# An LSTM over 512 steps: the output gate's columns computed last and in another PSUM bank, a head of 56 steps, no half cells

## The chip, the cores and the metric

The kernel runs on one core of a Trainium2 chip. A core has five engines with instruction queues of their own that run in order: TensorE (PE, with its weight loads PEld), VectorE (DVE), ScalarE (ACT), GpSimd (POOL) and SyncE (SP), which here starts nearly all DMAs. The metric is the device time of one execution in microseconds (us), lower is better. All data is 32-bit floating point.

## What is computed

An LSTM runs over x (32 sequences, 512 steps, 512 features) from a given state h0; its outputs are added to x. Wx and Wh are 512 x 2048, the four gates i, f, o and g of 512 columns each. Cut to what matters:

```python
xW = jnp.einsum('ntd,dg->ntg', x, Wx) + b
c0 = jnp.zeros_like(h0)

def step(carry, xw_t):
    prev_h, prev_c = carry
    a = xw_t + prev_h @ Wh
    i = jax.nn.sigmoid(a[:, :Hd])
    f = jax.nn.sigmoid(a[:, Hd:2 * Hd])
    o = jax.nn.sigmoid(a[:, 2 * Hd:3 * Hd])
    g = jnp.tanh(a[:, 3 * Hd:])
    next_c = f * prev_c + i * g
    next_h = o * jnp.tanh(next_c)
    return ((next_h, next_c), next_h)
```

The product x Wx does not depend on the recurrence, and can be computed ahead; h Wh can't.

## The kernel before, in words

**A step.** The gates of a step are a PSUM bank of 128 partitions by 512 columns: partition group j (32 partitions, the 32 sequences) holds 128 of each gate's 512 columns. `h_part` (L570) adds h Wh to it with 16 matmuls: four blocks k of the 512 rows by four column groups j of the array, each 512 columns wide; the four of one k run side by side. The trace has two records for each such matmul, for two passes. Two banks, `gates_0` and `gates_1`, alternate by step. `cell` (L592) then applies a sigmoid to i and f (L608), a tanh to g (L609), a sigmoid to o (L610) on ACT; f c, i g and their sum on DVE (L611 to L613); the tanh of c on ACT (L614); o times it on DVE (L615); and a transpose on DVE (L620), which gives ht, the stationary operand of the next `h_part`. POOL adds x for the output (L626). Before that, `seed_gates` (L560) has ACT copy xw, the finished x Wx + b of the step, into the bank, so that the matmuls accumulate on it.

**x Wx.** The first 8 steps are direct (`direct`, L522): 16 matmuls of 512 columns. Five of them run ahead of step 0, three in steps 0 to 2. Steps 8 to 31, the rest of the head (`HEAD`), are made in units (`UNITS`): a unit is 8 steps by 128 columns of each gate and takes, for both halves of the inner dimension, one level of a scheme with 7 products in place of 8. The remaining 480 steps are made in 20 superblocks of 24 steps, each by 20 outer products whose factors are sums of blocks of x and of Wx, and each outer product by the 7 inner ones. A product of the inner level is four matmuls of 256 columns side by side, called a set below: 14 sets make a unit, 140 a superblock.

**Factors.** 14 of the 20 right factors are sums of blocks of Wx. `make_factors` (L181) makes them on DVE in the first steps, two factors behind each cell in steps 0 to 4 and one after that, and SP stores them to memory; `fetch` (L683) loads them again for each superblock.

**Order.** All instructions are written out in a fixed order (L700 on) by time step k and window v; `windows_of(k)` is two windows for each of the first three steps and one for each after. A step issues, in this order: `h_part`; for its window the evacuations of earlier products (`evacuate`: copies on ACT, sums on DVE), planned DVE work (`run_due`), the window's products on PE, the DMAs of `fetch`; then the cell. `run_due` takes work from a list by due window, at most `ROOM` = 3400 columns in a window, each operation counted with 160 more, unless it is overdue. The products of a job are spread over five windows. Superblocks begin in window `START`, which is `LEAD` = 23 steps before the head's end; before this is step 9.

**Half cells.** From `SPLIT` (L551), once all products are made, steps run in halves: each half of the gates' columns has a bank of its own, and the cell is done once per half on half as many columns.

Of the kernel before, what the change touches and what calls it, by code (L numbers as in the profile page):

```python
# [19 lines left out]
H = P // 2  # L20
# [17 lines left out]
HEAD = 4 * ROW  # L38
# [19 lines left out]

START = windows_of(HEAD - LEAD)[0]

# [11 lines left out]
def kernel(  # L72
# [21 lines left out]
    gates = [psum.tile([P, 2, C], F32, name=f"gates_{i}") for i in range(2)]  # L94
# [7 lines left out]
    bias_sb = const.tile([P, 2, C], F32, name="bias_sb")  # L102
# [47 lines left out]
    load_row(3)  # L150
# [30 lines left out]
    def make_factors(n):  # L181
        wa, wb = ring(n, f"make_{n}")
        (first, s0), *rest = B_OF[n]
        assert s0 > 0
        ops = []
        for dst, part in ((wa[:, 0], slice(0, 1)), (wb[:, 0:3], slice(1, 4))):
            dst = dst if part.start else wa[:, 0:1]
            for m, (b, sign) in enumerate(rest):
                src = raw[first][:, part] if m == 0 else dst
                fn = nc.vector.tensor_add if sign > 0 else nc.vector.tensor_sub  # L190
                ops.append(lambda fn=fn, dst=dst, src=src, other=raw[b][:, part]: fn(dst, src, other))  # L191
        ops += [
            lambda: nc.vector.tensor_sub(wa[:, 1], wb[:, 0], wa[:, 0]),
            lambda: nc.vector.tensor_sub(wb[:, 3], wb[:, 2], wb[:, 0]),
            lambda: nc.vector.tensor_sub(wa[:, 2], wb[:, 2], wa[:, 1]),
            lambda: nc.vector.tensor_sub(wb[:, 0], wb[:, 1], wa[:, 2]),
            lambda: nc.sync.dma_start(out=kept[n][0], in_=wa.rearrange("p n c -> p (n c)")),
            lambda: nc.sync.dma_start(out=kept[n][1], in_=wb.rearrange("p n c -> p (n c)")),
        ]
        return ops  # L200

# [319 lines left out]

    def direct(t, bank, qs=range(4)):  # L522
        i, a = divmod(t, ROW)
        for q in qs:
            k, e = divmod(q, 2)
            for j in range(NJ):
                nc.tensor.matmul(
                    bank[j * B : (j + 1) * B].rearrange("p n c -> p (n c)"),
                    rows[i][:, a, q],
                    raw[NJ * k + j][:, 2 * e : 2 * e + 2].rearrange("p n c -> p (n c)"),  # L530
                    start=q == 0,
                    stop=True,
                    skip_group_check=True,
                )

    def keep_direct(t, bank):
        xw[t] = upool.tile([P, 2, C], F32, name=f"xw_{t}", tag="xw", bufs=4)
        nc.vector.tensor_add(xw[t], bank, bias_sb)  # L538

    def load_xw(t):  # L540
        xw[t] = upool.tile([P, 2, C], F32, name=f"xw_{t}", tag="xw", bufs=4)
        i, a = divmod(t, ROW)
        nc.sync.dma_start(out=xw[t].rearrange("p n c -> p (n c)"), in_=stored[i][a])
# [6 lines left out]
    last_window = START + PER * (NSB - 1) + begin(R - 1) + 5  # L550
    SPLIT = next(k for k in range(T) if windows_of(k - 1)[-1] > last_window)  # L551

    def is_split(t):
        return t >= SPLIT

    def half_of(t, i):
        pair = (pps[0], pps[1]) if (t - SPLIT) % 2 == 0 else gates
        return pair[i][:, 0]
# [11 lines left out]
    def h_part(t):  # L570
        if not is_split(t):
            order = [(None, k) for k in range(NJ)]
        else:
            order = [(i, k) for i, ks in ((0, (0, 1)), (1, (0,)), (0, (2, 3)), (1, (1, 2, 3))) for k in ks]
        for i, k in order:
            g = gates[t % 2].rearrange("p n c -> p (n c)") if i is None else half_of(t, i)
            cols = slice(0, 2 * C) if i is None else slice(i * C, (i + 1) * C)
            for j in range(NJ):
                nc.tensor.matmul(  # L579
                    g[j * B : (j + 1) * B],  # L580
                    state["ht"][:, k, :],
                    wh_sb[:, k, j, cols],
                    start=False,
                    stop=True,
                    skip_group_check=True,
                )
# [5 lines left out]
    def cell(t):  # L592
        n, tt = divmod(t, ROW)
        by_half = lambda a: a.rearrange("p (h u) -> p h u", u=H)
        s = work.tile([P, 2, G, H], F32, name=f"s_{t}", tag="s")
# [5 lines left out]
        two = is_split(t)  # L601
        for part in [slice(0, 1), slice(1, 2)] if two else [slice(0, 2)]:
            u = slice(H * part.start, H * part.stop)
            if two:
                g = half_of(t, part.start).rearrange("p (h g u) -> p h g u", h=1, g=G)
            else:
                g = gates[t % 2].rearrange("p h (g u) -> p h g u", g=G)
            nc.scalar.activation(s[:, part, 0:2], g[:, :, 0:2], AF.Sigmoid)  # L608
            nc.scalar.activation(s[:, part, 3], g[:, :, 3], AF.Tanh)  # L609
            nc.scalar.activation(s[:, part, 2], g[:, :, 2], AF.Sigmoid)  # L610
            nc.vector.tensor_mul(by_half(fc[:, u]), s[:, part, 1], by_half(state["c"][:, u]))  # L611
            nc.vector.tensor_mul(by_half(ig[:, u]), s[:, part, 0], s[:, part, 3])  # L612
            nc.vector.tensor_add(c[:, u], fc[:, u], ig[:, u])  # L613
            nc.scalar.activation(tc_t[:, u], c[:, u], AF.Tanh)  # L614
            nc.vector.tensor_mul(by_half(h[:, u]), s[:, part, 2], by_half(tc_t[:, u]))  # L615
            if t == T - 1:
                nc.vector.tensor_add(tc_t[:, u], h[:, u], state["x"][:, u])
                nc.sync.dma_start(out=out[n][:, tt * P + u.start : tt * P + u.stop], in_=tc_t[:, u])
                continue
            nc.vector.transpose(ht[:, 2 * part.start : 2 * part.stop].rearrange("p q b -> p (q b)"), h[:, u])  # L620
        if t == T - 1:
            return
        state["c"], state["ht"] = c, ht
        if tt % 2 == 0:
            state["oc"] = opool.tile([P, 2, NJ, B], F32, name=f"oc_{t}", tag="oc")
        (nc.gpsimd if not two else nc.vector).tensor_add(state["oc"][:, tt % 2], xr[t][:, tt % 2], ht)  # L626
# [9 lines left out]
    for u, (i, j) in enumerate(UNITS):  # L636
# [8 lines left out]
    def prepare(v):  # L645
# [3 lines left out]
        if job is None or job.w >= len(UNITS):  # L649
# [33 lines left out]
    def fetch(v):  # L683
# [9 lines left out]
        sb, rest = divmod(v + 6 - START, PER)  # L693
        if rest < MO and 0 <= sb < NSB:
            load_row(HEAD // ROW + MO * sb + (0, 2, 1)[rest])

    to_make = [n for n in range(R) if len(B_OF[n]) > 1]
    make_at = {k: 2 for k in range(5)}

    with tc.manual_schedule():  # L700
        warm = work.tile([P, G, P], F32, name="warm", tag="s")
        nc.scalar.activation(warm[:, 0], c_init, AF.Sigmoid)
        for m in range(10):
# [8 lines left out]
            bias_sb.rearrange("p n (m l) -> p (n m) l", l=B),  # L712
# [6 lines left out]
        for t in range(2):  # L719
            nc.vector.tensor_add(gates[t], gates[t], bias_sb)  # L720
        for t in range(2, 4):
            keep_direct(t, firsts[t])
        direct(4, pps[2])
        keep_direct(4, pps[2])
# [6 lines left out]
        for k in range(T):  # L731
# [7 lines left out]
            for m, v in enumerate(windows_of(k)):  # L739
                if v == START:  # L740
                    assert not to_make
# [71 lines left out]
```

## Time and profile before

| | us |
|---|---|
| median of 3 runs | 3269.84 (3269.76 to 3272.1) |
| the profiled execution | 3272.06 |
| its span, first to last instruction | 3270.2 |
| PE busy | 3163.7 |
| DVE busy | 2290.2 |
| ACT busy | 1473.4 |
| POOL busy | 931.3 |

The trace has one row per group of like instructions: the start and length in us, the engine, the line of the kernel and the operation, the tile written and those read, the shape, the count, and in brackets how long the engine was idle before and who released it. The end of a matmul in the trace is a model's, some 0.17 us behind the moment at which the next may start; so PE looks busier than it is. In the table of windows a row gives a stretch from a start to an end, its length, each engine's busy time with its count of instructions, the granted clock of TensorE, the share of the DMA engines and the rate.

### The profile page before, as it was taken

The page shows a single profiled execution, that of the slowest core. Times are in us where ns is not written, and L with a number is a line of the kernel's source. Part 1 is how long each engine was busy: PE and PEld are TensorE (multiplying, and loading weights), DVE is VectorE, ACT ScalarE, POOL GpSimd, SP SyncE. Part 2 cuts the span into 40 slices and gives each one's busy share as a digit, 9 for nine tenths or more (in the row PEclk, how much of TensorE's full clock was granted, in tenths as well). Part 3 has the DMA queues.
Part 4 walks back from the last instruction along what each step waited for, and adds up shares of the span by engine and source line. Part 5 has one row for each costly group of instructions (what it writes and reads, how often), then busy time and mean ns, then how long its engine had stood idle before and what let it go on. Part 6 is the DMA issues. An engine that isn't in the chain of part 4 may idle for free.

```text
span 3270.2 us, 101636 instructions
## 1 busy us (share of the span) xinstructions
PE 3163.7 (97%) x40980; PEld 1297.2 (40%) x40980; DVE 2290.2 (70%) x6388; ACT 1473.4 (45%) x4482; POOL 931.3 (28%) x1002
## 2 busy tenths in 40 slices
PE   7899999999999999999999999999999999999987
PEld 2334434434443434434443434444443434344333
DVE  4666776767676777767676777767676767767665
ACT  1344444444444444444444444444444444444434
POOL 0022332323232322323232323323232323323232
PEclk8999999999999999999999999999999999999999
DMA  4466566657566576666566565667566666666552
GB/s 181 157 192 223 179 221 204 221 180 236 182 211 225 171 227 196 221 194 225 177 221 209 191 222 186 219 198 232 171 222 203 200 217 183 220 207 223 174 158 69
DMA packets 324904, 649.79 MB, mean 199 GB/s; under 512 B 43600, under 2 KB 109264, under 8 KB 323920
## 3 DMA queue, kind: packets, MB, share of 16 engines
q1 hardware_dynamic: 324288, 643.28, 61.0%
q8 instruction: 322, 5.28, 0.7%
q14 instruction: 150, 1.23, 0.1%
q10 hardware_dynamic: 144, 0.01, 0.0%
HBM read 464.59 MB, written 178.52 MB: 197 GB/s over the span
## 4 chain that ended last, share of the span: by engine, by line
PE 75%; DVE 12%; issue 5%; ACT 5%; DMA 1%; POOL 1%; SPq 0%; DVEq 0%; ACTq 0%; POOLq 0%
PE gates L579 46%; PE pp L342 12%; PE acc L342 11%; PE p L342 4%; ACT s L608 2%; ACT ig L614 2%; DVE fc L611 2%; DVE ht L620 1%; DVE fc L615 1%; DVE c L613 1%; DVE ig L612 1%; POOL xw L546 1%; DVE wb_make L191 1%; DMA xw<-slot 1%; PE pp L579 1%
## 5 line engine op out<-in xcount | busy, mean ns | idle before, releaser
L579 PE MATMUL gates<-wh_sb,ht 128*32 128x512 f32 (+1 forms) x16352 | 1828.8, 588 | 49.0 <-DVE ht L620 42.1
L579 PEld LDWEIGHTS gates<-wh_sb,ht 128*32 128x32 f32 x16352 | 488.3, 109 | 1136.7 <-issue 883.3
L626 POOL TENSOR_TENSOR oc<-xr,ht 128x128 f32<-128x128 f32 x494 | 297.6, 602 | 2228.4 <-DVE ht L620 2228.4
L608 ACT ACTIVATE s<-gates 128x256 f32<-128x256 f32 (+1 forms) x512 | 194.2, 379 | 1119.3 <-PE gates L579 1119.1
L546 POOL TENSOR_TENSOR xw<-xw,bias_sb 128x512 f32<-128x512 f32 x504 | 651.7, 1294 | 96.1 <-DMA xw<-xw 44.6
L611 DVE TENSOR_TENSOR fc<-s,c 128x128 f32<-128x128 f32 (+1 forms) x529 | 155.7, 294 | 400.4 <-ACT s L608 396.6
L614 ACT ACTIVATE ig<-c 128x128 f32<-128x128 f32 (+1 forms) x530 | 162.0, 306 | 337.5 <-DVE c L613 337.5
L383 DVE TENSOR_TENSOR pp<-acc,p 128x256 f32<-128x256 f32 x412 | 177.7, 431 | 191.7 <-ACT pp L382 176.9
L615 DVE TENSOR_TENSOR fc<-s,ig 128x128 f32<-128x128 f32 (+1 forms) x530 | 153.3, 289 | 221.6 <-ACT ig L614 221.6
L381 ACT COPY pp<-pu 128x512 f32<-128x512 f32 x412 | 247.8, 601 | 125.5 <-DVE slot L489 63.0
L565 ACT COPY gates<-xw 128x512 f32<-128x512 f32 x492 | 285.1, 579 | 34.3 <-DVE xw L538 33.6
L342 PE MATMUL pp<-wb,node 128*32 128x256 f32 x3200 | 247.0, 379 | 0.0
L620 DVE STREAM_TRANSPOSE ht<-fc 128x128 f32<-128x128 f32 (+1 forms) x528 | 162.3, 307 | 56.9 <-DVE fc L615 3.7
L377 DVE TENSOR_TENSOR pu<-acc,p 128x256 f32<-128x256 f32 x412 | 168.8, 410 | 15.9 <-ACT p L374 11.8
L342 PE MATMUL acc<-wa,s 128*32 128x256 f32 x2240 | 173.6, 380 | 2.9
L342 PE MATMUL pp<-wb,s 128*32 128x256 f32 x2240 | 172.7, 379 | 0.0
L342 PE MATMUL acc<-wb,s 128*32 128x256 f32 x2240 | 172.7, 379 | 0.0
L342 PE MATMUL p<-wa,s 128*32 128x256 f32 x2240 | 172.7, 379 | 0.0
L382 ACT COPY pp<-acc 128x256 f32<-128x256 f32 x412 | 148.6, 361 | 43.6 <-DVE slot L489 24.9
L370 ACT COPY pu<-acc 128x256 f32<-128x256 f32 x412 | 151.7, 368 | 31.4 <-PE acc L342 31.4
L613 DVE TENSOR_TENSOR c<-fc,ig 128x128 f32<-128x128 f32 (+1 forms) x530 | 152.3, 287 | 18.4
L374 ACT COPY p<-p 128x256 f32<-128x256 f32 x412 | 154.7, 375 | 5.1 <-PE p L342 5.1
(136 smaller groups left out, 3806.4 us busy)
## 6 DMA issues: line engine op xcount, KB each, us to landing
wb<-keep_b SPq DMA_DIRECT2D x280, 512.0 KB, 5.4
xw<-xw SPq DMA_DIRECT2D x504, 256.0 KB, 3.9
wa<-keep_a SPq DMA_DIRECT2D x280, 384.0 KB, 4.7
xw<-slot SPq DMA_DIRECT2D x488, 128.0 KB, 3.3
xw<-t SPq DMA_DIRECT2D x268, 128.0 KB, 3.4
xr<-in_x_dram SPq DMA_DIRECT2D x256, 128.0 KB, 3.0
out_dram<-oc SPq DMA_DIRECT2D x255, 128.0 KB, 1.9
row<-in_x_dram SPq DMA_DIRECT2D x63, 512.0 KB, 6.6
```

The lines of the kernel that those rows point to most:

```text
L342: nc.tensor.matmul(dst[t * B : (t + 1) * B], a[:, t], w, start=s in (1, 5) and m == 0, stop=True, skip_group_check=True,)
L381: nc.scalar.copy(job.pp[0], job.pu)
L546: nc.gpsimd.tensor_add(xw[t], xw[t], bias_sb)
L565: nc.scalar.copy(gates[t % 2], xw[t])
L579: nc.tensor.matmul(g[j * B : (j + 1) * B], state["ht"][:, k, :], wh_sb[:, k, j, cols], start=False, stop=True, skip_group_check=True,)
L608: nc.scalar.activation(s[:, part, 0:2], g[:, :, 0:2], AF.Sigmoid)
L611: nc.vector.tensor_mul(by_half(fc[:, u]), s[:, part, 1], by_half(state["c"][:, u]))
L613: nc.vector.tensor_add(c[:, u], fc[:, u], ig[:, u])
L614: nc.scalar.activation(tc_t[:, u], c[:, u], AF.Tanh)
L615: nc.vector.tensor_mul(by_half(h[:, u]), s[:, part, 2], by_half(tc_t[:, u]))
L620: nc.vector.transpose(ht[:, 2 * part.start : 2 * part.stop].rearrange("p q b -> p (q b)"), h[:, u])
L626: (nc.gpsimd if not two else nc.vector).tensor_add(state["oc"][:, tt % 2], xr[t][:, tt % 2], ht)
```

## The change

Five things change together.

- The columns are laid out anew: i, f, g and o are now blocks of 128 columns of the bank, o last. `h_part` first runs the 16 matmuls over the 384 columns of i, f and g in bank `gates[t % 2]`, then 16 over the 128 columns of o, in bank `gates[(t + 1) % 2]`. The cell reads its gates from these two banks; its own operations are the same.
- The seed becomes two ACT copies: 384 columns for step k + 2 (`seed_first`) and 128 columns for step k + 1 (`seed_last`), both behind the cell of step k.
- `HEAD` grows from 32 to 56 steps: 24 units instead of 12 and 19 superblocks instead of 20. `START` moves from step 9 to step 33. The units stand in windows 0 to 36 by `UNIT_AT`: the first four in windows 0 to 3, the others spread.
- All 8 direct steps run ahead of step 0. The made factors come from `run_due`'s list (`push_factors`) with due windows spread over the head, and each stores both its parts in one entry. Rows of x from the fourth on are loaded by `fetch`.
- Half cells are gone: the last steps run as the others do, and in the last three DVE adds x in place of POOL.

```diff
-HEAD = 4 * ROW
+HEAD = 7 * ROW
...
+UNIT_AT = [u if u < NJ else NJ + (u - NJ) * (START - NJ - 1) // (len(UNITS) - NJ - 1) for u in range(len(UNITS))]
...
-    gates = [psum.tile([P, 2, C], F32, name=f"gates_{i}") for i in range(2)]
+    gates = [psum.tile([P, G * P], F32, name=f"gates_{i}") for i in range(2)]
...
+    def push_factors():
+        done = []
+        ops = [op for n in range(R) if len(B_OF[n]) > 1 for op in make_factors(n)]
+        for i, (columns, fn) in enumerate(ops):
+
+            def go(fn=fn):
+                fn()
+                done.append(fn)
+
+            push(2 + (START - 6) * i // len(ops), columns, go, lambda _, i=i: len(done) == i)
...
-    def seed_gates(t):
-        if is_split(t):
-            for i in range(2):
-                nc.scalar.copy(half_of(t, i), xw[t][:, i])
-        else:
-            nc.scalar.copy(gates[t % 2], xw[t])
+    def seed_first(t):
+        if t < T:
+            nc.scalar.copy(gates[t % 2][:, 0:IFG], xw[t][:, 0:IFG])
+
+    def seed_last(t):
+        if t < T:
+            nc.scalar.copy(gates[(t + 1) % 2][:, IFG:], xw[t][:, IFG:])
...
     def h_part(t):
-        if not is_split(t):
-            order = [(None, k) for k in range(NJ)]
-        else:
-            order = [(i, k) for i, ks in ((0, (0, 1)), (1, (0,)), (0, (2, 3)), (1, (1, 2, 3))) for k in ks]
-        for i, k in order:
-            g = gates[t % 2].rearrange("p n c -> p (n c)") if i is None else half_of(t, i)
-            cols = slice(0, 2 * C) if i is None else slice(i * C, (i + 1) * C)
...
+        for g, cols in ((gates[t % 2], slice(0, IFG)), (gates[(t + 1) % 2], slice(IFG, G * P))):
+            for k in range(NJ):
+                for j in range(NJ):
+                    nc.tensor.matmul(
+                        g[j * B : (j + 1) * B, cols],
+                        state["ht"][:, k, :],
+                        wh_sb[:, k, j, cols],
+                        start=False,
+                        stop=True,
+                        skip_group_check=True,
+                    )
...
+        g = gates[t % 2].rearrange("p (g u) -> p g u", u=P)
+        o = gates[(t + 1) % 2].rearrange("p (g u) -> p g u", u=P)[:, 3]
+        nc.scalar.activation(s[:, 0:2], g[:, 0:2], AF.Sigmoid)
+        nc.scalar.activation(s[:, 2], g[:, 2], AF.Tanh)
+        nc.scalar.activation(s[:, 3], o, AF.Sigmoid)
...
+        for t, bank in zip(range(4, ROW), (pps[2], accs[0], accs[1], p5)):
+            direct(t, bank)
+            keep_direct(t, bank)
+        seed_first(0)
+        seed_last(0)
+        seed_first(1)
+        push_factors()
...
                     cell(k)
-                    for _ in range(make_at.get(k, 1 if k < START else 0)):
-                        if to_make:
-                            for op in make_factors(to_make.pop(0)):
-                                op()
+                    seed_first(k + 2)
+                    seed_last(k + 1)
                 for op in prepare(v + 1):
                     op()
-                if m == 0 and k < 3:
-                    direct(k + 5, gates[k % 2])
-                    keep_direct(k + 5, gates[k % 2])
-                if m == 0 and k + 2 < T:
-                    seed_gates(k + 2)
```

More of the change, by code (lines that the diff above doesn't have):

```diff
@@ L200, in make_factors, with add, keep @@
-        return ops
+                def add(part=part, m=m, b=b, fn=v.tensor_add if sign > 0 else v.tensor_sub):
+                    to = dst(part)
+                    fn(to, to if m else raw[first][:, part], raw[b][:, part])
+                ops.append(((part.stop - part.start) * C, add))
+        def keep():
+            for to, part in zip(kept[n], tiles):
+                nc.sync.dma_start(out=to, in_=part.rearrange("p n c -> p (n c)"))
+        ops += [
+            (C, lambda: v.tensor_sub(tiles[0][:, 1], tiles[1][:, 0], tiles[0][:, 0])),
+            (C, lambda: v.tensor_sub(tiles[1][:, 3], tiles[1][:, 2], tiles[1][:, 0])),
+            (C, lambda: v.tensor_sub(tiles[0][:, 2], tiles[1][:, 2], tiles[0][:, 1])),
+            (C, lambda: v.tensor_sub(tiles[1][:, 0], tiles[1][:, 1], tiles[0][:, 2])),
+            (0, keep),
+        ]
@@ L740 @@
                 if v == START:
-                    assert not to_make
+                    assert len(due) == 0 or due[0][0] >= START
                     free.extend(t.rearrange("p (h n) c -> p h (n c)", h=2) for t in others)
```

117 lines of the change are left out of this document (43 added, 74 removed).

## The prediction

> **What bounds the kernel now.** I read the page first, then the stretches of the run in a table of windows, then one step in order of time. From the page:
>
> ```profile
> span 3270.2 us, 101636 instructions
> PE 3163.7 (97%) x40980; PEld 1297.2 (40%) x40980; DVE 2290.2 (70%) x6388; ACT 1473.4 (45%) x4482; POOL 931.3 (28%) x1002
> L579 PE MATMUL gates<-wh_sb,ht 128*32 128x512 f32 (+1 forms) x16352 | 1828.8, 588 | 49.0 <-DVE ht L620 42.1
> ```
>
> PE looks full, but its ends are modelled, so 97% proves nothing; the stretches do better (columns: length, then busy us and count for PE, PEld, DVE, ACT, POOL, then clock, DMA share, GB/s):
>
> ```profile
> 34.60:183.90 149.30, 118.18 (x1572) 51.29 (x1568) 101.28 (x224) 38.33 (x106) 10.92 (x13) 0.87 0.42 139
> 183.90:334.40 150.50, 149.06 (x1956) 60.46 (x1952) 97.41 (x282) 72.22 (x214) 40.27 (x47) 1.00 0.64 207
> 334.40:3147.30 2812.90, 2776.50 (x35873) 1132.46 (x35868) 2014.93 (x5625) 1315.22 (x3952) 848.81 (x912) 1.00 0.64 205
> 3147.30:3180.10 32.80, 23.60 (x236) 7.71 (x224) 15.97 (x40) 9.68 (x32) 10.26 (x10) 0.95 0.43 129
> 3180.10:3270.20 90.10, 66.13 (x1152) 36.51 (x1152) 51.51 (x198) 35.97 (x176) 20.87 (x17) 0.99 0.23 72
> ```
>
> These are steps 0 to 8, 9 to 32, 33 to 488 (19 periods of 24), 489 to 493 and 494 to 511. A plain step issues 32 L579 records (16 matmuls, two passes each), and the third stretch alone, filtered to that line, has this row:
>
> ```profile
> 334.40:3147.30 2812.90, 1659.64 (x14592) 434.02 (x14588) 1.00 0.64 205
> ```
>
> 14592/32 = 456 steps, so 148.05 us per 24 and 6.17 per step. One such step:
>
> ```profile
> 1605.00 0.16 PEld L579 LDWEIGHTS gates<-wh_sb,ht 128*32 128x32 f32 x8 [0.34 <-DVE ht L620]
> 1605.00 3.64 PE L579 MATMUL gates<-wh_sb,ht 128*32 128x512 f32 x32
> 1605.46 0.13 PEld L579 LDWEIGHTS gates<-wh_sb,ht 128*32 128x32 f32 x4 [0.30 <-issue]
> 1605.89 0.13 PEld L579 LDWEIGHTS gates<-wh_sb,ht 128*32 128x32 f32 x4 [0.30 <-issue]
> ...
> 1608.46 0.61 PE L342 MATMUL acc<-wa,s 128*32 128x256 f32 x8
> 1608.71 0.38 ACT L608 ACTIVATE s<-gates 128x256 f32<-128x256 f32 x1 [2.96 <-PE gates L579]
> 1608.89 0.61 PE L342 MATMUL pp<-t,node 128*32 128x256 f32 x8
> 1609.12 0.29 DVE L611 TENSOR_TENSOR fc<-s,c 128x128 f32<-128x128 f32 x1 [1.49 <-ACT s L608]
> 1609.15 0.28 ACT L610 ACTIVATE s<-gates 128x128 f32<-128x128 f32 x1
> 1609.65 0.29 DVE L613 TENSOR_TENSOR c<-fc,ig 128x128 f32<-128x128 f32 x1
> 1610.04 0.31 ACT L614 ACTIVATE ig<-c 128x128 f32<-128x128 f32 x1 [0.61 <-DVE c L613]
> 1610.19 0.61 PE L342 MATMUL p<-wa,s 128*32 128x256 f32 x8
> 1610.78 0.31 DVE L620 STREAM_TRANSPOSE ht<-fc 128x128 f32<-128x128 f32 x1
> 1611.15 2.35 PE L579 MATMUL gates<-wh_sb,ht 128*32 128x512 f32 x20 [0.35 <-DVE ht L620]
> ```
>
> Matmuls go in groups of four. The loads' starts show one group of 512 columns per 0.43 us; L342 shows two groups of 256 in (1610.19 - 1608.46)/4 = 0.432. So a group costs its columns, with no fixed part that 0.01 us shows. h Wh takes 3.46, then the first sigmoid starts 0.25 after its stream, and the next h Wh 2.44 after the sigmoid: 3.46 + 0.25 + 2.44 = 6.15. PE's products (five sets of 0.432 here, mostly six) end at 1610.62 and PE truly idles 0.53. **The cell's chain sets the step**; PE's own work for 24 steps is 24 x 3.44 + 140 x 0.432 = 143.0 against 148.05.
>
> **The change part by part.** *Output gate apart.* h Wh becomes 8 groups of 384 columns (8 x 0.3225 = 2.58), then 8 of 128. The three first gates are complete 0.85 earlier: the sigmoid of i and f starts at 0.03 (first loads exposed, 0.46 - 0.43) + 2.58 + 0.25 = 2.86 and ht is there for PE at 2.86 + 2.44 = 5.30. The new wait of ACT is the sigmoid of o, which queues ahead of the tanh of c. o ends near 3.48 on PE, so that sigmoid runs about 3.73 to 4.01; the tanh was due 1.33 after the first sigmoid (1610.04 - 1608.71), at 4.19. Covered by 0.18 us; without the cover the overrun goes straight into the chain. The o matmuls wait for ACT's seed of 128 columns, issued behind the previous cell, 2.6 us before it is needed; the products queue behind them. Two seed copies instead of one add one small ACT instruction of about 0.2 (fixed parts of the rows above), on an engine 45% busy that waited 2.96 before this sigmoid.
>
> *The price nobody can read off.* No group of 128 columns stands in the trace. Column-proportional it is 0.109; from above, the nearest row with as many matmuls and loads is a group of 256, 0.216. What could lift it are the four loads: their row spans 0.13, longer than 0.107 of streaming. But eight loads span only 0.16, so one more group of loads costs 0.03; I take 0.109, since 256 columns show no trace of loads either. Then h Wh is 2.58 + 0.87 = 3.45, as before, and PE's step is 3.45 + 6 x 0.432 = 6.04, or 5.61 with five sets, both later than the chain's 5.30. **PE becomes the bound**: 24 x 3.45 + 60.5 = 143.3 per 24 steps.
>
> The Trainium skill speaks against this: "TensorE: Matmul & The Clock Gate", section "Back-to-back issue gap", gives streams of load and matmul pairs at 128 columns about 81 ns each where matmuls alone take 56. An estimate from those two figures is 25 ns more per group, 0.134, which by my sum below would leave about nothing of the gain. The spacing at 256 columns here shows no such surcharge, and no row tests it at 128.
>
> *DVE's queue.* It is unchanged in these steps and in some ends too late for 5.30:
>
> ```profile
> 1808.06 3.64 PE L579 MATMUL gates<-wh_sb,ht 128*32 128x512 f32 x32
> 1811.84 0.16 PEld L342 LDWEIGHTS acc<-wa,s 128*32 128x32 f32 x8 [1.05 <-DVE pp L383]
> 1814.46 3.62 PE L579 MATMUL gates<-wh_sb,ht 128*32 128x512 f32 x32
> 1818.14 0.29 DVE L305 TENSOR_TENSOR s<-node 128x128 f32<-128x128 f32 x1
> 1820.58 0.64 PE L579 MATMUL gates<-wh_sb,ht 128*32 128x512 f32 x4
> ```
>
> The first (6.40) has products waiting on DVE; in the second DVE ends at 1818.43, 3.97 after the start, and DVE alone would give about 6.0. I leave about 1.5 us per 24 steps with DVE: 144.8. Gain 148.05 - 144.8 = 3.25, times 19 = **-62**. The first four of these steps carry 31 sets of leftover units instead of 23: **+3**.
>
> *The head.* All 14 made factors now go through the planned list, and 24 units instead of 12 are spread to window 36. Before, they choked the first steps:
>
> ```profile
> L191 DVE TENSOR_TENSOR wb_make<-wb_make,raw 128x768 f32<-128x768 f32 x17 | 16.3, 958 | 0.6
> PE acc L342 <- DVE pp L383: 21.3, 5, 6.4
> 34.57 5.84 PE L579 MATMUL gates<-wh_sb,h_init 128*32 128x512 f32 x32
> 42.83 3.61 PE L527 MATMUL gates<-raw,row 128*32 128x512 f32 x32
> 334.44 1.04 PE L579 MATMUL gates<-wh_sb,ht 128*32 128x512 f32 x8
> ```
>
> Steps 0 and 33 start at 34.6 and 334.4. PE waited 21.3 for DVE in between, and the granted clock of the stretch above was 0.87. After: directs 5 to 7 (L527) move ahead of step 0, 3 x 3.44 = 10.3, which puts step 0 at 34.6 + 10.3 = 44.9. In the changed program's order of instructions stand 64 sets of 256 columns in steps 0 to 2 and 252 in steps 3 to 32. From step 3 on DVE has at most 4.9 us ahead of a cell (0.96 for 768 columns as in the first row, the other shapes alike), and some 2 of the cell itself, below PE's time for that step in each of them. So PE sets both parts: 3 x 3.45 + 64 x 0.432 = 38, plus 9 allowed for a cold clock and evacuations at two windows per step; then 30 x 3.45 + 252 x 0.432 = 212.4. Step 33 starts at 304.3 instead of 334.4: **-30**. Bounds: 9 less, or nothing gained. Loads of row 3 and the stores of factors move later in SP's queue; what follows them there (residuals, sums for a step three later) has a step of cover, and a landing that slipped past it would add its few us once or twice.
>
> *The end.* Half cells go: steps 494 to 511 took 90.1, 5.0 each with all their stalls; at 5.30 they take 95.4, **+5**. Steps 489 to 493 took 32.8 for few products; two at 6 and three at 5.3 give 28, **-5**. PE's gaps of 1.8 there are shorter than the 2.6 after which this stretch lost its clock:
>
> ```profile
> 3166.08 3.64 PE L579 MATMUL gates<-wh_sb,ht 128*32 128x512 f32 x32 [2.17 <-DVE ht L620]
> 3172.30 5.34 PE L579 MATMUL gates<-wh_sb,ht 128*32 128x512 f32 x32 [2.58 <-DVE ht L620]
> ```
>
> If it is lost all the same, each such step costs 1.7 (5.34 - 3.64).
>
> Sum: -62 + 3 - 30 + 5 - 5 = -89 on the span of 3270.2; I give back 4 for stalls of a PE that now has no slack, -85. The profiled execution took 3272.1, 2.2 over the median of the runs, 3269.8; from the median it is **3185**.
>
> **The rivals.** *Loads not hidden at 128 columns* (slower): each group pays its loads' 0.03, 0.139 in all, 0.24 per step. PE's 24 steps are 149.1, with DVE's share about 149.6, 1.5 over before: 19 x 1.5 = +29; the head keeps -30 + 33 x 0.24 = -22; with +3 it is +10, **3280**. For it: a load row is longer than the stream it must hide behind. Against: 256 columns hide it wholly, eight loads take 0.16. It decides from about 0.025 us per group on, where 8 x 0.025 x 420 PE-bound steps (33 and five of six in 456, with the end) eat the 85. The skill's rule above is this case.
>
> *A group of 128 costs as one of 256* (issue-bound): +0.85 per step; 24 x 0.85 - 1.5 = 18.9 per period over 144.8, or 19 x 18.9 = +359, head +28, end about +9: -85 + 396, **3581**. For it: the instructions are as many. Against: eight loads started within the 0.16 row, so issue is no slower than 0.02 each.
>
> *The steps don't shorten*, because DVE's queue, not the sigmoid, releases the cell: then only head, +3 and end count, -27, **3243**. Against: L611 above waited 1.49 for ACT with DVE idle.
>
> **How the numbers follow.** Forecast 0.65 with its own range 3165 to 3215; loads 0.17, issue 0.08, unshortened steps 0.10. Slower than 3276 (by over 0.2%, about what a measurement of this kernel can tell) are 0.14 of the loads' case and all of the issue's, 0.22; within 0.2% lie the other 0.03 of loads and 0.02 of the unshortened steps; the rest is faster, 0.73. The range runs from 3160 (no stalls in the head, less left with DVE) to 3285 (loads); only the issue case and strays lie outside.
>
> **What would show it.** Right: loads of consecutive 128-column groups about 0.11 apart; waits of L579's successor on ht nearly gone from steps 33 to 488; steps of 6.05 and 5.6; step 33 near 304. Wrong: 128-column groups at 0.13 or more; ht still the releaser; the sigmoid of o starting after c is ready; PE waiting on L383's successor all over the head.

## The result

| | before | after |
|---|---|---|
| median, us | 3270.97 (4 runs, 3269.76 to 3273.13) | 3182.93 (4 runs, 3179.14 to 3184.11) |
| the profiled execution, us | 3272.06 | 3179.14 |
| its span, us | 3270.2 | 3177.3 |

The ratio is 0.9728 (95% interval 0.9711 to 0.9745): 88.0 us less between the medians, 92.9 between the two profiled spans; the profiled execution of after is the fastest of its four.

From the page of after: the totals, the chain that ended last by engine, and the costliest group:

```profile
span 3177.3 us, 134411 instructions
PE 3120.9 (98%) x57012; PEld 2035.9 (64%) x57012; DVE 2209.9 (70%) x6155; ACT 1626.0 (51%) x4890; POOL 937.8 (30%) x1017
PE 91%; DVE 5%; ACT 2%; DMA 1%; issue 1%; SPq 0%; DVEq 0%
L596 PE MATMUL gates<-wh_sb,ht 128*32 128x384 f32 x32704 | 1874.3, 379 | 38.8 <-DVE ht L631 35.5
```

The chain line of before's page for comparison:

```profile
PE 75%; DVE 12%; issue 5%; ACT 5%; DMA 1%; POOL 1%; SPq 0%; DVEq 0%; ACTq 0%; POOLq 0%
```

PE's busy share says little (97% before, 98% now). The chain says more: PE carries 91% of it instead of 75%, and the cell's engines, DVE and ACT, have fallen from 17% to 7%. The kernel has gone from a chain through the cell to a bound by PE's own work.

The table of windows of after, cut at the same steps as before's (up to step 0; steps 0 to 32; 33 to 488; 489 to 493; 494 to 511):

```profile
0.00:44.20 44.20, 39.83 (x310) 11.81 (x314) 10.71 (x24) 3.20 (x6) 0.20 (x4) 1.00 0.62 234
44.20:309.10 264.90, 254.87 (x4645) 163.16 (x4641) 153.51 (x389) 114.58 (x332) 53.02 (x61) 0.99 0.49 154
309.10:3051.60 2742.50, 2738.70 (x50535) 1810.52 (x50531) 2004.81 (x5611) 1466.30 (x4413) 848.13 (x912) 1.00 0.66 210
3051.60:3078.90 27.30, 21.65 (x388) 12.68 (x381) 15.10 (x40) 10.83 (x34) 9.53 (x11) 1.00 0.53 156
3078.90:3177.30 98.40, 65.89 (x1152) 37.71 (x1152) 25.80 (x93) 31.13 (x105) 26.96 (x32) 1.00 0.21 66
```

Set beside the rows of before, the whole difference is accounted for:

| stretch | before | after | measured | predicted |
|---|---|---|---|---|
| up to step 33 | 334.4 | 309.1 | -25.3 | -30 |
| steps 33 to 488 | 2812.9 | 2742.5 | -70.4 | -62 + 3 |
| steps 489 to 493 | 32.8 | 27.3 | -5.5 | -5 |
| steps 494 to 511 | 90.1 | 98.4 | +8.3 | +5 |
| given back for stalls | | | | +4 |
| sum | 3270.2 | 3177.3 | -92.9 | -85 |

One steady step of after in order of time (start, length, engine, line and operation, tiles, shape, count; in brackets the idle time before and its releaser):

```profile
1598.36 3.67 PE L596 MATMUL gates<-wh_sb,ht 128*32 128x384 f32 x64
1598.69 0.16 PEld L596 LDWEIGHTS gates<-wh_sb,ht 128*32 128x32 f32 x4 [0.17 <-issue]
1599.01 0.16 PEld L596 LDWEIGHTS gates<-wh_sb,ht 128*32 128x32 f32 x4 [0.17 <-issue]
...
1600.94 0.81 PEld L596 LDWEIGHTS gates<-wh_sb,ht 128*32 128x32 f32 x28 [0.17 <-issue]
1601.21 0.39 ACT L619 ACTIVATE s<-gates 128x256 f32<-128x256 f32 x1 [1.50 <-PE gates L596]
...
1602.14 0.28 ACT L621 ACTIVATE s<-gates 128x128 f32<-128x128 f32 x1 [0.38 <-PE gates L596]
...
1602.48 0.29 DVE L624 TENSOR_TENSOR c<-fc,ig 128x128 f32<-128x128 f32 x1
...
1602.81 0.31 ACT L625 ACTIVATE ig<-c 128x128 f32<-128x128 f32 x1 [0.39 <-DVE c L624]
...
1603.55 0.31 DVE L631 STREAM_TRANSPOSE ht<-fc 128x128 f32<-128x128 f32 x1
...
1603.97 0.64 PE L367 MATMUL pp<-wb,s 128*32 128x256 f32 x8
```

The next step starts at 1604.41, 6.05 after this one. The groups of 384 columns stand 0.32 apart (1598.69, 1599.01). Seven loads of groups of 128 come as one row of 28 in 0.81; less the last group's 0.16 that is six spacings of 0.108. The sigmoid of i and f (L619) starts 2.85 after the step, before the o columns are done, and ht is finished at 1603.86, while PE still has products to run until 1604.40 (the last set starts at 1603.97 and a set is 0.43). So in this step ht is no longer what PE waits for. Over the whole stretch, PE's groups by line:

```profile
L596 PE MATMUL gates<-wh_sb,ht 128*32 128x128 f32 (+1 forms) x29333 | 1681.1, 379 | 3.8 <-DVE ht L631 2.2
```

Between 305 and 3060 us PE idled 3.8 us in all ahead of h Wh; the same row of before, over its steps 33 to 493, has 40.4:

```profile
L579 PE MATMUL gates<-wh_sb,ht 128*32 128x512 f32 x14752 | 1679.5, 595 | 40.4 <-DVE ht L620 40.3
```

A step at the end of after, where no products are left, shows the cell's chain by itself:

```profile
3100.26 3.66 PE L596 MATMUL gates<-wh_sb,ht 128*32 128x384 f32 x64 [1.68 <-DVE ht L631]
...
3104.04 0.28 ACT L621 ACTIVATE s<-gates 128x128 f32<-128x128 f32 x1 [0.38 <-PE gates L596]
3104.06 0.29 DVE L624 TENSOR_TENSOR c<-fc,ig 128x128 f32<-128x128 f32 x1
3104.38 0.31 ACT L625 ACTIVATE ig<-c 128x128 f32<-128x128 f32 x1
...
3105.61 0.85 PE L596 MATMUL gates<-wh_sb,ht 128*32 128x384 f32 x8 [1.68 <-DVE ht L631]
```

The chain takes 5.35 here, and PE idles 1.68 for it. The new wait, the sigmoid of o, ends at 3104.32, 0.06 before the tanh of c starts; in the median of steps 33 to 488 it is 0.06 as well.

### The profile page after: what moved, and what is told of

It is laid out like the page before. It is cut to its first block, busy times and chain, and to the rows that moved or that the text cites. A ratio compares the mean times of both kernels' runs of the same rounds, so it can differ in the third digit from the quotient of the medians.

```text
span 3177.3 us, 134411 instructions
## 1 busy us (share of the span) xinstructions
PE 3120.9 (98%) x57012; PEld 2035.9 (64%) x57012; DVE 2209.9 (70%) x6155; ACT 1626.0 (51%) x4890; POOL 937.8 (30%) x1017
## 4 chain that ended last, share of the span: by engine, by line
PE 91%; DVE 5%; ACT 2%; DMA 1%; issue 1%; SPq 0%; DVEq 0%
PE gates L596 52%; PE acc L367 16%; PE pp L367 16%; PE p L367 5%; DMA xw<-slot 1%; ACT ig L625 0%; DVE c L624 0%; DVE fc L626 0%; DVE fc L622 0%; DVE ht L631 0%; DVE node L302 0%; ACT pp L406 0%; SPq L424 0%; PE pp L712 0%; PE pp L555 0%
## 5 line engine op out<-in xcount | busy, mean ns | idle before, releaser
L596 PE MATMUL gates<-wh_sb,ht 128*32 128x384 f32 x32704 | 1874.3, 379 | 38.8 <-DVE ht L631 35.5
L596 PEld LDWEIGHTS gates<-wh_sb,ht 128*32 128x32 f32 x32704 | 1131.4, 110 | 794.2 <-issue 659.0
L619 ACT ACTIVATE s<-gates 128x256 f32<-128x256 f32 x512 | 196.8, 384 | 777.7 <-PE gates L596 777.6
L408 DVE TENSOR_TENSOR pp<-acc,p 128x256 f32<-128x256 f32 x404 | 174.6, 432 | 275.5 <-ACT pp L407 261.6
L622 DVE TENSOR_TENSOR fc<-s,c 128x128 f32<-128x128 f32 x511 | 150.1, 294 | 203.9 <-ACT s L619 200.3
L626 DVE TENSOR_TENSOR fc<-s,ig 128x128 f32<-128x128 f32 x512 | 149.6, 292 | 192.7 <-ACT ig L625 192.7
L583 ACT COPY gates<-xw 128x384 f32<-128x384 f32 x508 | 240.3, 473 | 20.9 <-DVE xw L569 20.7
L621 ACT ACTIVATE s<-gates 128x128 f32<-128x128 f32 x512 | 142.0, 277 | 189.0 <-PE gates L596 188.8
L625 ACT ACTIVATE ig<-c 128x128 f32<-128x128 f32 x512 | 158.7, 310 | 139.1 <-DVE c L624 113.7
L631 DVE STREAM_TRANSPOSE ht<-fc 128x128 f32<-128x128 f32 x511 | 159.1, 311 | 54.6 <-DVE fc L626 0.9
L395 ACT COPY pu<-acc 128x256 f32<-128x256 f32 x404 | 150.3, 372 | 58.5 <-PE acc L367 51.3
```

Source lines behind the costliest of these rows:

```text
L408: nc.vector.tensor_add(job.pp[1][:, 1], job.acc, job.p5)
L583: nc.scalar.copy(gates[t % 2][:, 0:IFG], xw[t][:, 0:IFG])
L596: nc.tensor.matmul(g[j * B : (j + 1) * B, cols], state["ht"][:, k, :], wh_sb[:, k, j, cols], start=False, stop=True, skip_group_check=True,)
L619: nc.scalar.activation(s[:, 0:2], g[:, 0:2], AF.Sigmoid)
L625: nc.scalar.activation(tc_t, c, AF.Tanh)
L631: nc.vector.transpose(ht.rearrange("p q b -> p (q b)"), h)
```

## The experiments

Each edits the kernel after unless it says otherwise, and is compared with runs of the kernel before on the same chip. "Period" is 24 steps, the mean of 19.

**One bank and one stream again (e1).** Everything else of the change stays; h Wh runs as 16 matmuls of 512 columns again, o beside the others.

```diff
-        for g, cols in ((gates[t % 2], slice(0, IFG)), (gates[(t + 1) % 2], slice(IFG, G * P))):
+        for g, cols in ((gates[t % 2], slice(0, G * P)),):
...
-            nc.scalar.copy(gates[t % 2][:, 0:IFG], xw[t][:, 0:IFG])
+            nc.scalar.copy(gates[t % 2], xw[t])
...
-            nc.scalar.copy(gates[(t + 1) % 2][:, IFG:], xw[t][:, IFG:])
+            pass
...
-        o = gates[(t + 1) % 2].rearrange("p (g u) -> p g u", u=P)[:, 3]
+        o = gates[t % 2].rearrange("p (g u) -> p g u", u=P)[:, 3]
```

> The changed kernel with the output gate's columns put back beside the others: 16 matmuls of 512 columns in one bank, one seed copy; the new head and the steps without halves stay. Theory (the sigmoids that start earlier release PE, nothing else does in steps 33 to 488): a period of 24 returns from 144.3 to 148.05, 19 x 3.7 = +71, and the 21 steps at the end from 5.34 to 6.15, +17; span near 3265. Rival (the steps got shorter by what the head change moved, such as the stores and loads of factors): the period stays near 144.3 and the span near 3180 to 3195.

Measured: 3261.44 us (8 runs, 3260.36 to 3263.44), ratio 0.997 (0.996 to 0.998): without the split the change is worth 0.3%. That is a balance. Beside before, this run reaches step 33 earlier by 24.2 (310.2 against 334.4), takes 18.7 less in steps 33 to 488 and 0.5 less in the next five, and loses 34.5 in the last 18, where it has neither the split nor half cells. The theory's direction held, but its span of 3265 was met partly by luck: of the +71 expected in steps 33 to 488 51.7 came, and in place of +17 at the end 31.2 over steps 489 to 511. Its windows of steps 33 to 488 and 494 to 511, and three of its last steps on PE:

```profile
310.20:3104.40 2794.20, 2764.07 (x35943) 1135.04 (x35939) 2004.59 (x5611) 1318.40 (x3957) 846.79 (x912) 1.00 0.64 206
3136.70:3261.30 124.60, 76.46 (x576) 21.85 (x576) 25.79 (x93) 26.32 (x88) 26.93 (x32) 0.90 0.16 51
```

```profile
3162.95 5.33 PE L596 MATMUL gates<-wh_sb,ht 128*32 128x512 f32 x32 [2.55 <-DVE ht L631]
3170.84 3.64 PE L596 MATMUL gates<-wh_sb,ht 128*32 128x512 f32 x32 [2.56 <-DVE ht L631]
3177.03 5.11 PE L596 MATMUL gates<-wh_sb,ht 128*32 128x512 f32 x32 [2.55 <-DVE ht L631]
```

The split is worth 2794.2 - 2742.5 = 51.7 in the steady steps and 124.6 - 98.4 = 26.2 at the end. In the end steps nothing covers the cell: with one stream PE idles 2.55 in each step, and in about every second step its clock is lost (5.33 and 5.11 instead of 3.64), so steps of 6.19 alternate with some of 7.7 to 7.9. With the split the same gap is 1.7, the clock is 1.00 and each step takes 5.34. The other 2812.9 - 2794.2 = 18.7 of the steady gain is not the split's, and the traces show where it sits. In before, 19 of each 24 steps have a separate semaphore instruction of ACT ahead of the tanh of c, which then starts 0.094 behind c in the median (1609.94 to 1610.04 in the step shown ahead); e1 has none there, and its tanh starts 0.033 behind c in every phase, as here:

```profile
1608.22 0.29 DVE L624 TENSOR_TENSOR c<-fc,ig 128x128 f32<-128x128 f32 x1
1608.54 0.31 ACT L625 ACTIVATE ig<-c 128x128 f32<-128x128 f32 x1 [0.55 <-DVE c L624]
```

Over 19 x 19 steps 0.061 makes 22, of which the first period of e1, with its leftover units, takes some 3 back. Which edit took the instruction away is not shown. With the split, the 0.061 would lie on a chain that PE's work covers, so how the 70.4 divides depends on the order in which the parts are added; the split alone on top of before was not run.

**Every group 128 columns wide (e2), and o as two streams of 64 (e3).** The work is the same, in 32 and 24 groups instead of 16.

```diff
-        for g, cols in ((gates[t % 2], slice(0, IFG)), (gates[(t + 1) % 2], slice(IFG, G * P))):
+        for g, cols in [(gates[t % 2], slice(c, c + P)) for c in (0, P, 2 * P)] + [(gates[(t + 1) % 2], slice(IFG, G * P))]:
```

```diff
-        for g, cols in ((gates[t % 2], slice(0, IFG)), (gates[(t + 1) % 2], slice(IFG, G * P))):
+        for g, cols in [(gates[t % 2], slice(0, IFG))] + [(gates[(t + 1) % 2], slice(c, c + P // 2)) for c in (IFG, IFG + P // 2)]:
```

> The first three gates' 384 columns as three rounds of 128 as well, so that h Wh is 32 groups of 128 columns and PE has 64 matmuls more records in a step. Theory (a group costs its columns and a fixed 2.7 ns, from 322.6 for 384 and 109.3 for 128 columns): 16 groups more, 0.04 us per step, +19 in all, span near 3196. Rival (loads or issue bind in a long run of 128 columns, 0.13 us a group or more): 24 x 0.02 = +0.5 us per step or more, over +210, span over 3390.

> The output gate's 128 columns as two rounds of 64. Theory (columns and a fixed 2.7 ns): 0.056 us a group, 16 groups 0.90 instead of 8 groups 0.87, +0.02 us per step, about +10, span near 3187. Rival (below 128 columns the four loads of a group bind, their row spans 0.13 and eight span 0.16): between 0.08 and 0.13 us a group, +0.4 to +1.2 us per step, span 3350 to 3700.

Measured: e2 3428.08 (4 runs, 3425.86 to 3434.57), ratio 1.0483 (1.0465 to 1.0502); e3 3226.6 (2 runs), ratio 0.9865 (0.9845 to 0.9885). Both forecasts were too low. e2 lands where its rival put it, over 3390, but not for the rival's reason: the price of a group did not change. A whole h Wh at the end of e2, 32 groups of 128:

```profile
3383.15 3.70 PE L596 MATMUL gates<-wh_sb,ht 128*32 128x128 f32 x128 [1.68 <-DVE ht L631]
```

That is 3.70 against 3.66 for the 16 groups of after's end step. Sixteen groups more cost 0.04, and the starts of records give the same: 0.3226 per group of 384, 0.216 of 256, 0.1093 of 128, 0.056 of 64, which is 0.000833 per column and 0.0027 fixed (16 x 0.0027 = 0.043). So the loss is not in the groups. It is in a wait that after doesn't have; PE's waits in e2, with total, times and longest:

```profile
PE gates L596 <- issue: 110.6, 102, 3.2
...
PE acc L367 <- issue: 26.4, 24, 2.5
```

With those ahead of other products (14.0 and 3.8) these are 154.8 us in 142 waits for which no other engine is the releaser; e3 has 20.0 of them, after none among its PE waits. They fall where much has just been issued, as here in e2:

```profile
1709.27 0.59 PE L367 MATMUL pp<-t,node 128*32 128x256 f32 x2
1711.70 0.42 PE L367 MATMUL pp<-t,node 128*32 128x256 f32 x3 [1.84 <-issue]
```

A set is cut in the middle. The instruction queue's row of after's and of e2's page (packets, MB, share):

```profile
q8 instruction: 449, 7.36, 1.0%
```

```profile
q8 instruction: 705, 11.55, 1.4%
```

e2 has 256 packets more than after and 16 x 4 x 2 x 512 = 65536 PE records more (16 more groups of four records, a matmul and a load each, in 512 steps): one packet of 16 KB holds 256 instructions. I formed a new theory from this: the instructions arrive too slowly. Worked out from the records, 256 of them in a row go in at the fastest in 6.05 us in after (6.27 in its steady steps), 4.35 in e3 and 3.42 in e2. All 168 waits of e2 and e3 end 1.1 to 1.6 after an instruction packet has landed, though these packets land 4.6 (e2) and 5.4 (e3) apart in the median. The Trainium skill, "Runtime: NRT & Kernel Launch", section "Instruction fetch mechanics", has the same blocks of 256 instructions and calls the cost of a crossing mostly hidden. These runs agree with the block and, if the waits are the fetch's, not with the hiding.

**The first three gates as 256 and 128 columns (e10).** The new theory's test: as many instructions as in e3, but no group narrower than 128, as in after.

```diff
-        for g, cols in ((gates[t % 2], slice(0, IFG)), (gates[(t + 1) % 2], slice(IFG, G * P))):
+        for g, cols in ((gates[t % 2], slice(0, 2 * P)), (gates[t % 2], slice(2 * P, IFG)), (gates[(t + 1) % 2], slice(IFG, G * P))):
```

> The three gates as one round of 256 columns and one of 128, then the output gate's 128: as many matmuls per step (48) as with the output gate in two rounds of 64, but no group under 0.109 us. Fixed cost of 8 groups more: 0.02 us per step, +9. Theory (PE waits for instructions, which come 256 at a time, when 256 of them are used up in less than about 5 us; the number of matmuls in a step decides): issue gaps again, some 10 to 40 us in all, span 3195 to 3225. Rival (only runs of groups of 0.06 us starve PE): no issue gaps, span near 3186.

Measured: 3216.63 (4 runs, 3213.33 to 3226.41), ratio 0.9836 (0.9816 to 0.9856), beside e3 and not beside after. Its period is 146.3 against e3's 146.7, after's 144.3 and e2's 156.8. It has 577 packets like e3, and the same kind of wait, 14.3 us in all, of which the largest row:

```profile
q8 instruction: 577, 9.45, 1.2%
```

```profile
PE acc L367 <- issue: 8.1, 8, 2.0
```

All 18 of these waits end 1.3 to 1.6 after a packet has landed, and the waits (10 to 40 forecast) and the span of 3215.3 (3195 to 3225) lie in the theory's ranges. So the number of PE instructions in a step decides, not their width: with six sets, matmuls and loads together, 224 in after, 288 in e3 and e10, 352 in e2. In e10 256 of them go in at the fastest in 5.02 us. That the fetch is what is late is the reading that fits the packets and the waits' places; it was not shown by changing the fetch. The waits and the forecast cost of the added groups make 23 of the 38 us by which e10's span exceeds after's, 30 of 47 in e3 and 174 of 251 in e2. Each wait is also some 0.2 longer than its row says, since the ends of matmuls are modelled, and e2's mean clock is 0.991 against 0.999; the rest was not taken apart.

**The head: 32 steps (e4), 80 steps (e9), factors due earlier (e5).**

```diff
-HEAD = 7 * ROW
+HEAD = 4 * ROW
```

> The changed kernel with a head of 32 steps again (12 units, 20 superblocks, start at step 9), factors still through the planned list. Theory (the longer head pays because it gives DVE time for the factors): DVE has some 70 us ahead of the cells of steps 1 to 4 and step 9 starts near 173; 20 x 144.2 + 3 gives step 489 at 3060, span near 3186, +9. Rival (the plan alone cured the head, its length only costs PE 12 us of products more): span near 3165, -12.

```diff
-HEAD = 7 * ROW
+HEAD = 10 * ROW
```

> The changed kernel with a head of 80 steps (36 units, 18 superblocks). Theory (with the factors covered, PE sets the head as it sets the rest, and every set counts): 24 steps by units take 24 x 14 - 140 = 28 sets of 0.432 more (12 units, 168 sets, for 140), +12; DVE's late steps fall away in one period, -1; span near 3188. Rival (the longer a head, the better, since DVE and the DMAs have less to do in it): span at or under 3177.

```diff
-            push(2 + (START - 6) * i // len(ops), columns, go, lambda _, i=i: len(done) == i)
+            push(1 + 8 * i // len(ops), columns, go, lambda _, i=i: len(done) == i)
```

> The changed kernel, but all operations that make factors have due windows 1 to 8 instead of 2 to 33, so DVE has to make them in steps 0 to 4 as the kernel before did; the units and the longer head stay. Theory (the head's gain is DVE no longer standing in front of the cells of the first steps): DVE has 62 us ahead of the cells of steps 1 to 4 instead of 26; step 5 starts near 130 instead of 111, and the span grows by about 19, to near 3196. Rival (the head gained because its units are spread, and factors were covered): span within 4 of 3177.

Measured: e4 3198.26 (4 runs, 3195.69 to 3201.02), ratio 0.9779 (0.9764 to 0.9793); e9 3196.38 (4 runs, 3193.9 to 3197.64), 0.9767 (0.9752 to 0.9782); e5 3212.85 (4 runs, 3210.86 to 3215.52), 0.9813 (0.98 to 0.9826). All three lose, from 13 to 30 us against after's median. PE's wait for DVE's sums of products, in after, e4 and e5:

```profile
PE acc L367 <- DVE pp L408: 5.0, 2, 2.5
```

```profile
PE acc L367 <- DVE pp L408: 16.5, 3, 7.6
```

```profile
PE acc L367 <- DVE pp L408: 13.2, 3, 5.6
```

And the windows from step 0 to step 5 in after and in e5:

```profile
44.20:111.00 66.80, 57.57 (x996) 31.72 (x988) 39.22 (x99) 22.74 (x65) 2.21 (x5) 0.95 0.33 108
```

```profile
45.00:140.50 95.50, 68.95 (x996) 34.69 (x988) 83.09 (x183) 22.46 (x65) 2.20 (x5) 0.82 0.46 166
```

The same 996 matmul records take 28.7 longer in e5, because DVE has 83.09 to do in that stretch instead of 39.22, and PE's waits lower its clock to 0.82, which lengthens its own work as well. In e5 step 33 then starts at 339.1, later than before's 334.4. The theories' directions held. By the medians e4, e5 and e9 lie 15, 30 and 13 above after, where 9, 19 and 12 had been expected, so the size fits in e9 and was too small in the other two. In e9 PE sets the head: a head of 24 steps more replaces one superblock (140 sets) by 12 units (168 sets), 28 x 0.432 = 12.1 of PE work. Steps 33 to 56, which the units now make, take 161.4 there, 17.3 more than a period of after without leftover units (144.2); the 5 beyond the 12.1 were not taken apart. So the long head pays once, because it takes the factors off the first steps, and not a second time.

**The one bias add beside DVE (e8).** The longest step of a period of after takes 6.38 in the median, more than its products; here one of 6.45, from 1772.19 to 1778.64:

```profile
1775.01 1.32 POOL L577 TENSOR_TENSOR xw<-xw,bias_sb 128x512 f32<-128x512 f32 x1 [2.52 <-DMA xw<-slot]
...
1775.10 1.38 DVE L332 TENSOR_TENSOR s<-row 128x128 f32<-128x128 f32 x1
...
1776.60 0.28 DVE L622 TENSOR_TENSOR fc<-s,c 128x128 f32<-128x128 f32 x1
```

L332 takes 1.38 beside POOL's bias add, 0.28 else, and the first DVE operation of the cell (L622) is pushed to 1.56 behind its sigmoid at 1775.04. In 18 of the 19 periods some DVE operation of this step is stretched by 0.4 or more, always beside a bias add. POOL had waited for a late load of xw, issued at 1769.00 and landed at 1774.85 (its row names another DMA). e8 issues those loads one step earlier, with five buffers for xw and three for pu.

```diff
-LEAD = 23
+LEAD = 24
...
-            job.pu = upool.tile([P, 2, C], F32, name=f"pu_{job.w}", tag="pu", bufs=4)
+            job.pu = upool.tile([P, 2, C], F32, name=f"pu_{job.w}", tag="pu", bufs=3)
...
-    def load_xw(t):
-        xw[t] = upool.tile([P, G * P], F32, name=f"xw_{t}", tag="xw", bufs=4)
+    def load_xw(t):
+        xw[t] = upool.tile([P, G * P], F32, name=f"xw_{t}", tag="xw", bufs=5)
...
-            if 2 * 4 - 3 <= k and k + 3 < T:
-                load_xw(k + 3)
+            if k == 5:
+                load_xw(8)
+            if 5 <= k and k + 4 < T:
+                load_xw(k + 4)
```

> The changed kernel with the finished sums of a step loaded one step earlier (five buffers instead of four, one of the four buffers of evacuated products given up for it, superblocks started one step earlier). Theory (in two or three steps of 24 POOL's add of the bias waits for its load, then runs beside DVE's sums ahead of the cell and holds one of them 1.4 us instead of 0.28): these steps fall from 6.38 and 6.32 to about 6.05 to 6.2, 19 x 0.4 = -8, span 3169. Rival (DVE's own queue sets these steps): no change, 3177.

Measured: 3185.21 (5 runs, 3184.09 to 3189.14), ratio 0.9731 (0.9717 to 0.9744): no change beside after. That step did fall, from 6.38 to 6.04 in the median, but the next rose from 6.32 to 6.60 and another from 6.04 to 6.26, and the period is 144.45. In that step no DVE operation of e8 is stretched in any period, so its cause was right. What rose has another: in the step of 6.26, in 14 of 18 periods DVE now waits, up to 1.5, for a store of finished sums that frees its slot, as here:

```profile
1615.54 0.69 DVE L514 TENSOR_TENSOR slot<-t,pp 128x512 f32<-128x512 f32 x1 [0.78 <-DMA xw<-slot]
```

After has no such wait in that step. In the step of 6.60 nothing is stretched either; DVE's L408, ahead of its sums, starts 2.21 into the step in the median instead of 1.92. Whether the earlier loads or the buffer taken from pu did this was not tested apart.

**Half cells at the end, on top of the change (e6), and the bias on DVE there (e7).** From step 494 on, the cell runs in two halves of 64 columns of each gate, each with a bank of its own; POOL no longer adds x there, and in e7 it does not add the bias either.

```diff
+    def h_halves(t):
+        for i, ks in ((0, (0, 1)), (1, (0,)), (0, (2, 3)), (1, (1, 2, 3))):
+            for k in ks:
+                for j in range(NJ):
+                    nc.tensor.matmul(
+                        half_of(t, i)[j * B : (j + 1) * B],
+                        state["ht"][:, k, :],
+                        of_half(wh_sb[:, k, j], i),
...
-        (nc.gpsimd if t < T - 3 else nc.vector).tensor_add(state["oc"][:, tt % 2], xr[t][:, tt % 2], ht)
+        (nc.gpsimd if not two else nc.vector).tensor_add(state["oc"][:, tt % 2], xr[t][:, tt % 2], ht)
```

and in e7 also

```diff
-        nc.gpsimd.tensor_add(xw[t], xw[t], bias_sb)
+        (nc.gpsimd if t < SPLIT + 2 else nc.vector).tensor_add(xw[t], xw[t], bias_sb)
```

> The changed kernel with the last 18 steps in half cells as before (halves of each gate, two banks each, DVE adds x, POOL adds the bias). Theory (without products the chain sets the step; two half chains overlap): 5.0 us per step as before instead of 5.34, some pairs lengthened where POOL's add of the bias meets DVE; span 3177 - 6 = 3171. Rival (the separate output gate is worth as much as halves): no change, 3177.

> As the run with half cells, but DVE adds the bias in these steps, so POOL runs nothing there. Theory (the steps over 4.4 us before were DVE held while POOL ran; 4.41 undisturbed): 18 x (5.34 - 4.41) = -17, span 3160. Rival (DVE's 0.65 for the bias lands in the chain): 18 x 0.6 of it is given back, 3171.

Measured: e6 3175.16 (4 runs, 3173.41 to 3177.19), ratio 0.9698 (0.9684 to 0.9711); e7 3167.24 (4 runs, 3166.43 to 3170.55), ratio 0.9675 (0.9662 to 0.9688). The windows of the last 18 steps, e6 and e7:

```profile
3084.40:3174.90 90.50, 66.21 (x1152) 40.27 (x1152) 51.30 (x198) 35.97 (x176) 20.77 (x17) 0.99 0.23 72
```

```profile
3085.00:3168.80 83.80, 65.90 (x1152) 40.75 (x1152) 50.70 (x214) 36.65 (x176) 0.81 (x1) 0.98 0.25 77
```

90.5 and 83.8 instead of after's 98.4: 7.9 and 14.6 less, where 6 and 17 had been expected. What e6 leaves on the table is again POOL beside DVE, here in the chain itself:

```profile
3139.81 2.54 POOL L578 TENSOR_TENSOR xw<-xw,bias_sb 128x512 f32<-128x512 f32 x2 [7.34 <-DMA xw<-xw]
...
3141.13 1.30 DVE L662 TENSOR_TENSOR ig<-s 128x64 f32<-128x64 f32 x1
```

L662 takes 0.22 on average in e7, and steps there are 4.40 apart, which two of its PE rows show:

```profile
3129.20 3.66 PE L613 MATMUL pp<-wh_sb,ht 128*32 128x256 f32 x64 [0.74 <-DVE fc L661]
3133.59 3.66 PE L613 MATMUL gates<-wh_sb,ht 128*32 128x256 f32 x64 [0.74 <-DVE fc L661]
```

The Trainium skill, "SBUF — State Buffer", section "Who interferes with whom", has VectorE operations with two inputs in SBUF contend with GpSimd's reads; the traces agree, with 1.30 and 1.38 instead of 0.22 and 0.28. e7 is faster than both kernels, about 15 us below after's median (in ratios to the same kernel before: 0.9675 against 0.9728, and the intervals do not touch).

## Why the prediction was right

The time was 3182.93 against 3185, each term had the right sign, and the mechanism is the one named. That the time came within about 2 us is partly luck, since misses of 3 to 11 us in the terms offset each other. By its steps:

- **A group of 128 costs 0.109.** It does: 0.1093. Of the two slower rivals, loads that don't hide (0.139) and a group as dear as one of 256 (0.216), neither happened. The estimate of 0.134 from the two figures of the Trainium skill ("TensorE: Matmul & The Clock Gate", section "Back-to-back issue gap") does not hold for these groups. The same section's other formula, columns / 2.4 + 2.5 ns, is by my estimate 109.2 ns if the columns of both passes (256) are put in, which is what the starts show.
- **The sigmoid at 2.86, ht for PE at 5.30.** The sigmoid came at 2.85. The chain alone is seen in the end steps, where no product hides it: 5.34 per step. The cover of o's sigmoid is thinner than the 0.18 forecast: 0.06 in the end steps, where DVE has no other work, and in the median of the steady ones. In the steady step above DVE's queue makes it 0.39 (L621 ends at 1602.42, L625 starts at 1602.81, behind c). About half of what is missing is the tanh of c, which starts 0.06 sooner behind c than in before (the semaphore instruction of e1's section); the rest is the sigmoid itself, which ends at 4.06 of the step instead of 4.01. The new wait was free, with little to spare.
- **PE becomes the bound, steps of 6.04 and 5.61.** Their medians are 6.043 for six sets and 5.612 for five. This killed the rival in which DVE releases the cell and steps don't shorten; e1 shows the split's worth directly.
- **1.5 us per 24 steps left with DVE.** Too much. Three steps of 24 are longer than PE's work, 6.38, 6.32 and 6.20 instead of 6.04, 0.8 in all, and the period came to 144.3 instead of 144.8. With 19 periods and the allowance for leftover units this is the term that was mis-sized: -59 forecast, -70.4 measured. Of it 51.7 go with the split when it is taken away (e1), and 18.7 are there without it; the forecast booked the whole to the split, and did not see that the tanh of c would start sooner.
- **The head, -30.** It was -25.3. Step 0 came at 44.19 (44.9 forecast), and steps 3 to 32 took 213.6 (212.4 forecast). Steps 0 to 2 took 15.7 + 17.4 + 18.2 = 51.3 instead of 47: the allowance of 9 for clock and evacuations was 4 too small. e4 and e5 show what was at stake there: with fewer steps to spread the factors over, or with them due early, step 33 starts 16 and 30 later (325.6 and 339.1).
- **The end, +5.** It was +8.3: 17 steps of 5.34 are 90.8, and the last step with its output takes 7.6, which the forecast had counted as a step like the others. The clock stayed at 1.00 with gaps of 1.7, as forecast, and e1 shows the other side, gaps of 2.55 and a clock of 0.90.
- **The 4 given back** was not needed, since PE found few stalls. In the spans, these 4 and the steady steps' 11 outweigh the 5 missed in the head and the 3 at the end; that makes 92.9 against 85. Between the medians, which differ less than the two profiled executions, it is 88.

## What to carry to other kernels

When a chain and an engine's own work are nearly equal, look for the operand that the chain needs last and compute it last, into a place that lets the rest be read already: taking that away again in e1 cost 84 of the 92.9 us of span, 26 of them in the last 18 steps, which have no half cells any more. Narrower matmuls cost little more than their columns (0.0027 a group) until waits with no releaser appear, here with 288 PE instructions in a step of 6.06 us but not with 224 in 6.04, so count instructions per stretch of time before cutting work finer. Once an engine without slack sets the pace, look at what it waits for in the few longest steps, and at whether one engine's operation stretches another's: taking POOL off the chain's end brought 6.7 us (e7 beside e6, last 18 steps), moving loads nothing (e8).

## What the runs showed of the hardware

- **PE waits that follow instruction packets.** With 256 PE records in a row going in no faster than 6.05 us there was no wait without a releaser; at 5.02 (e10) and 4.35 (e3) there were 14.3 and 20.0 us of them in the run, at 3.42 (e2) 154.8. All end 1.1 to 1.6 after an instruction packet has landed. That the supply of instructions causes them is inferred.
- **The clock and short gaps.** In e1, gaps of 2.55 in steps of about 6.2 cost the clock in 8 of the last 18 steps (5.33 for a stream of 3.64); gaps of 1.68 in after's end steps of 5.34 never did.
- **POOL beside DVE.** A DVE operation of 0.22 to 0.28 took 1.30 to 1.38, about the length of the POOL operation beside it (1.27 to 1.32).
